# Layer 2 of a four-layer graph network: weights times values by one level of Strassen's method

## The chip, the cores and the metric

The kernel runs on one core of one Trainium2 chip. The metric is the device time of one execution in microseconds (us), smaller being better. Several executions were timed; one more was profiled.

In the profile PE is TensorE's matmul, PEld its weight load (which runs beside PE), DVE is VectorE, ACT is ScalarE, POOL is GpSimd and SP is SyncE, whose queue issues nearly all DMAs here. L977 is line 977 of the kernel before.

## What is computed

A graph of N = 3327 nodes with 256 features each goes through four layers. Each layer adds its output to its input and normalizes the rows. All arithmetic is f32. Layer 2, cut to what matters:

```python
q = x @ Wq.T + bq
k = x @ Wk.T + bk
v = x @ Wv.T + bv
scores = q @ k.T / sqrt(256)
scores = where(adj > 0, scores, -9e15)
attention = softmax(scores, axis=-1)
att = attention @ v
x = layernorm(x + elu(att))
```

Layers 0, 1 and 3 have the same core, a masked softmax of N x N weights times N x 256 values. Layer 0's weights come from a cosine similarity. In layer 1, and in the three graph attention layers that make up layer 3 (called 3a, 3b and 3c in the kernel), a weight comes from a sum of one term per row and one per column, without a matmul of scores.

## The kernel before

N is padded to 26 tiles of 128 nodes. The queries are cut into 7 blocks b: six of 512 (four tiles) and a last one of 256 (two tiles). The main loop goes over steps (layer, b, j), j being one of the 26 tiles of keys.

For each step, `make` builds the weights of tile j against block b, a tile e of 128 keys x 512 queries. In layer 2 that is `weights2` (line 489 on): two calls of the score matmul (line 498, 512 columns each), an exp on ACT (line 506) and a multiplication by the 0/1 mask on DVE (line 425, in `masked`). In the graph attention layers it is a Relu on ACT (line 591) and an operation on DVE (line 599). `make` runs LA = 2 steps ahead of the products.

The products are line 977: for each of the block's four query tiles k, the 128 x 128 part of e is the stationary operand and V[j], 128 keys x 257 columns, streams past it into PSUM. Column 257 of V is 1, so that the last column of the result is the sum of the weights. The four results `pos` lie in one PSUM bank each, from a pool of five banks (`ps_o`); three more banks (`ps_b`) serve scores and everything else. A block adds up over its 26 tiles of keys.

When a block is done, `finish` divides by the sum (lines 720 to 724: a max and a reciprocal on DVE, a scaling on ACT), applies the nonlinearity, adds the input, normalizes, and prepares what the next layer needs. It is a generator: the main loop advances it one piece per step, so that this work lies beside the next block's products. In layer 1 it also turns the rows (a DMA transpose), and computes the values of layer 2 with the matmul of line 846. A generator `block2` computes the query side of the next block of layer 2 (`gT`) from j = 14 on. `Sum` gathers the mean of the values, which is written into the row of the one padded node at the end of a layer (lines 639 to 647).

The masks of a block, 1.7 MB, are fetched by one DMA per block. The setups of layers (`setup1`, `setup2`, `setup3a`, `setup3`) load and combine weight matrices; `setups` runs them in pieces during layer 0 from block 1 on.

Past the first four steps, the tile framework's scheduler orders the instructions of each engine by its own estimates, so the order on an engine isn't that of the source. Buffers come from pools: a tag with `bufs=n` has n buffers, and a new tile waits until its buffer's last user is done. Among the tags concerned, `x4k` has two buffers, shared by xT, gT, the transposes' planes and pT4; `e` has five; `acc` has one.

Of the kernel before, what the change touches and what calls it, by code (L numbers as in the profile page):

```python
# [8 lines left out]
F32 = mybir.dt.float32  # L9
# [21 lines left out]

@with_exitstack
def gnn_stack(ctx: ExitStack, tc: tile.TileContext, a: dict, N: int, out: bass.AP):

# [53 lines left out]
    for k in range(4):  # L90
        nc.tensor.matmul(turned[:, :P], count, part, start=(k == 0), stop=(k == 3))
    ident = const.tile([P, P], F32, name="ident")
    nc.vector.tensor_tensor(ident, turned[:, :P], count, ALU.is_equal)
    ispad = ident[:, P - 1 : P]
    notpad = const.tile([P, 1], F32, name="notpad")
    nc.vector.tensor_scalar(notpad, ispad, -1.0, 1.0, ALU.mult, ALU.add)


    V = [
# [7 lines left out]

    s_d = [dram.tile([1, bw(b)], F32, name=f"s_d{b}") for b in range(NB)]
    a_d = {k: dram.tile([1, 4 * P], F32, name=f"a_d{k}") for k in ("1", "3a", "3b", "3c")}
    x_d = {  # L110
        k: [dram.tile([P, D], F32, name=f"x{k}_d{t}") for t in range(NT)]
        for k in ("2", "3c")
# [45 lines left out]
    def gat_rows(key, wt, v):  # L158

        c = wts.tile([P, 4], F32, tag="wa", name="wa")  # L160
        nc.scalar.copy(
            c.rearrange("p (i f) -> p f i", i=2),
            times(wt, v).rearrange("p (f i) -> p f i", i=2),
        )
        yield
        pr = bank("prt")
        nc.tensor.transpose(pr[:4, :P], c, ident)
        rt = wts.tile([4, P], F32, tag="rt", name="rt")
        nc.scalar.copy(rt, pr[:4, :P])
        nc.sync.dma_start(a_d[key].rearrange("o (c n) -> (o c) n", n=P), rt)  # L170
        r = wts.tile([P, 2, D], F32, tag="row_" + key, name="row_" + key)
        nc.sync.dma_start(
            r.rearrange("p i n -> p (i n)"),
            a_d[key].rearrange("o n -> (o n)").partition_broadcast(P),
        )
        w["row_" + key] = r
# [71 lines left out]
        yield  # L248
        yield from gat_rows("3a", w0t, c)

    def setup3(key, n):
        w[key] = load_w(f"l3_w{n}")
        wt = load_w(f"l3_w{n}t", wts, "scratch1")
        v = load_a(key)
        yield
        yield from gat_rows(key, wt, v)

    def setups():
        for g in (setup1(), setup2(), setup3a(), setup3("3b", 2), setup3("3c", 3)):
            yield from g  # L260
            yield

# [120 lines left out]
    def take_adj(b, j):  # L383

        wd = bw(b)
        st = stages.pop((b, j))[:, : 2 * wd]
        nc.vector.tensor_scalar(mask(b, j, 2), st, 0, None, ALU.is_gt)  # L387
        if j == 0:
            adj_sum[b] = st
        elif j == 2:  # L390
            acc = work.tile([P, 2 * CH], I32, tag="acc", name="acc", bufs=1)
            acc = acc[:, : 2 * wd]
            nc.vector.tensor_tensor(acc, adj_sum[b], st, ALU.add)
            adj_sum[b] = acc
        else:
            acc = adj_sum[b]
            nc.vector.tensor_tensor(acc, acc, st, ALU.add)  # L397
# [209 lines left out]
            return e  # L607


    def turn(x4, n, out):  # L610

        half = "p k (n t) -> p t k n"
        pl = work.tile([P, 4, 2, D], U16, tag="x4k", name="planes", bufs=2)
        for t in range(2):
            nc.scalar.copy(pl[:, :n, t, :], x4[:, :n, :].bitcast(U16).rearrange(half, t=2)[:, t])  # L617
        yield
        tr = work.tile([P, 16, P], U16, tag="stage", name="turned", bufs=3)
        nc.sync.dma_start_transpose(  # L620
            out=tr[:, : 4 * n, :], in_=pl[:, :n].rearrange("p k t n -> p (k t n)")
        )
        for _ in range(3):
            yield
        trv = tr[:, : 4 * n, :].rearrange("p (k t h) i -> p t k h i", t=2, h=2)
        for t in range(2):
            nc.vector.tensor_copy(out(t), trv[:, t])  # L627
        yield
# [19 lines left out]
    def finish(L, b, pos):  # L648
# [21 lines left out]
        if L.key == "0":  # L670
# [15 lines left out]

            z0 = cols.tile([P, 4], F32, tag="z0", name="z0")
            nc.vector.tensor_scalar(z0[:, :n], z_[:, :n], 0.1, None, ALU.is_lt)
            if b == NB - 1:
                nc.vector.tensor_tensor(  # L690
                    z0[:, n - 1 : n], z0[:, n - 1 : n], notpad, ALU.mult
                )
            c2 = cols.tile([P, 4], F32, tag="c2", name="c2")
            nc.vector.tensor_scalar(c2[:, :n], am, -1.0, 2.0, ALU.mult, ALU.add)
            for k, t in enumerate(ts_):
# [19 lines left out]
                    yield  # L715
        else:
            p4 = work.tile([P, 4, D], F32, tag="stage", name="p4", bufs=3)
            for k, t in enumerate(ts_):
                ri = cols.tile([P, 1], F32, tag="ri", name="ri", bufs=4)
                nc.vector.tensor_scalar(  # L720
                    ri, pos[k][:, D : D + 1], TINY, None, ALU.max
                )
                nc.vector.reciprocal(ri, ri)
                nc.scalar.mul(p4[:, k, :], pos[k][:, :D], ri)  # L724
            if L.key in x_d:
                x4 = work.tile([P, 4, D], F32, tag="stage", name="x4", bufs=3)
                xr = [x4[:, k, :] for k in range(4)]
# [77 lines left out]
        if not L.hidden:  # L805
# [29 lines left out]
            if L.key == "1":  # L835
# [7 lines left out]
                for k, t in enumerate(ts_):  # L843
                    pm = bank("pv")
                    for h in range(2):
                        nc.tensor.matmul(  # L846
                            pm[:, :D],
                            FT[b][:, h, k * P : (k + 1) * P],
                            w["v"][:, h, :],
                            start=(h == 0),  # L850
                            stop=(h == 1),
                        )
                    nc.vector.tensor_tensor(nxt[t][:, :D], pm[:, :D], w["bv"], ALU.add)
                    if k % 2:
                        yield
                dsts = [nxt[t][:, :D] for t in ts_]
            for k in range(0, n, 2):
                follow((k, k + 1), dsts)
# [3 lines left out]
            L.gat_next.rows(b)  # L862
        if b == NB - 1:
            L.sum.close(nxt[NT - 1])
            if L.gat_next is not None:
                L.gat_next.keys(ts_[0], NT)
        elif b == NB - 2 and L.gat_next is not None:
            L.gat_next.shift(ts_[-1] + 1)
            yield
            L.gat_next.keys(0, ts_[-1] + 1)  # L870
# [36 lines left out]
    def make(s):  # L907
        if s >= len(steps):
            return
        L, b, j = steps[s]  # L910
        if L.is_gat:
            made.append(L.gat.weights(b, j))
        else:
            made.append((weights0 if L.key == "0" else weights2)(b, j))

    for i in range(2):
        for t in range(NT):
# [21 lines left out]
    for s, (L, b, j) in enumerate(steps):  # L939
        last = L.key == "3c"  # L940
        first = L.key == "0" and b == 0
        if j == 0:
            pos = [
                ps_o.tile([P, D + 1], F32, tag="po", name="po") for _ in tiles_of(b)
            ]
        if first:

            g, part = (j + 4) // 4, j % 4
# [24 lines left out]
            next(prep[0])  # L973
        else:
            make(s + LA)
        for k in range(len(pos)):
            nc.tensor.matmul(  # L977
                pos[k],
                made[0][:, k * P : (k + 1) * P],
                V[L.i % 2][j],  # L980
                start=(j == 0),
                stop=(j == NT - 1),
            )
        made.popleft()
        if s == 3:
            start.__exit__(None, None, None)
        if L.key == "0" and j == NT - 1 - LA:
# [5 lines left out]
        elif j == 8 and not (last and b == NB - 1):  # L993
            nb = (b + 1) % NB
            masks[nb] = fetch_mask(nb)
        if L.key == "0" and b >= 1 and j % 3 == 1:
            next(setup, None)
        nl, nb = (L, b + 1)
        if nb == NB:
# [87 lines left out]
```

## Time and profile before

| what | us |
|---|---|
| median of 3 runs | 2434.77 |
| lowest and highest | 2433.78, 2436.84 |
| span of the profiled execution | 2434.4 |
| DVE, ACT busy | 1411.9, 1008.5 |
| products of line 977, PE busy, all layers (8112 records) | 1841.6 |
| scores of line 498, PE busy (728 records) | 320.4 |
| first and last score record of layer 2 start at | 847.6, 1454.0 |

The profile notes each f32 matmul call as two records, each with its own weight load. The length of a record on PE is modelled and longer than its share of the time, since matmuls overlap: 380 ns for a record of 257 columns. The distance from one record's start to the next is the time that it costs.

The granted TensorE clock was 0.995 of full speed over the span. In the 40 slices of the page PE is at nine tenths or more in all but the first and the last.

### The profile page before, as it was taken

The numbers are of one execution on the slowest core, as the hardware profiler recorded it, in microseconds if no ns is written. First come the engines' busy times: TensorE is split into PE (matmuls) and PEld (weight loads), VectorE is DVE, ScalarE is ACT, GpSimd is POOL, SyncE is SP. The second block draws the span as 40 slices with busy tenths as digits, with TensorE's granted clock in tenths as the row PEclk, the third lists the DMA queues.
The fourth block names the chain that finished last, engine by engine and source line by source line (L and its number), as shares of the span: only waits on it lengthen the run. The fifth ranks groups of instructions, "written<-read, shape, count | busy, mean of one in ns | idle before, by whom it ended". The sixth has DMA issues, their size and how long they took to land.

```text
span 2434.4 us, 27870 instructions
## 1 busy us (share of the span) xinstructions
PE 2397.5 (98%) x10117; PEld 1901.3 (78%) x10117; DVE 1411.9 (58%) x3625; ACT 1008.5 (41%) x1692; POOL 5.4 (0%) x65
## 2 busy tenths in 40 slices
PE   8999999999999999999999999999999999999997
PEld 6777777788888766666666688888888888888886
DVE  7567776666666634244244256655656655655665
ACT  4422222255555422222222245555465555655553
POOL 0000000000000000000000000000000000000000
PEclk9999999999999999999999999999999999999999
DMA  8145434222221301011010021111121111123121
GB/s 277 65 141 162 132 101 135 100 76 71 68 59 52 90 13 46 5 50 46 1 46 32 1 71 54 42 49 52 48 70 50 42 42 58 46 83 84 59 60 26
DMA packets 119998, 164.67 MB, mean 68 GB/s; under 512 B 73149, under 2 KB 97972, under 8 KB 115252
## 3 DMA queue, kind: packets, MB, share of 16 engines
q1 hardware_dynamic: 119588, 162.63, 21.6%
q8 instruction: 79, 1.29, 0.2%
q14 instruction: 59, 0.48, 0.1%
q10 hardware_dynamic: 272, 0.26, 0.0%
HBM read 124.72 MB, written 21.36 MB: 60 GB/s over the span
## 4 chain that ended last, share of the span: by engine, by line
PE 95%; DVE 3%; DMA 1%; issue 0%; ACT 0%; DVEq 0%; ACTq 0%
PE po L977 70%; PE ps L498 12%; PE ps L436 5%; PE pproj L765 4%; PE pv L846 1%; PE pgq L457 1%; DMA stage<-in_adj_a 1%; PE pqk L306 0%; DVE acc L397 0%; DVE ejunk L525 0%; DVE mask L387 0%; DVE e L425 0%; DVE e L599 0%; DMA turned<-planes 0%; PE pqkT L347 0%
## 5 line engine op out<-in xcount | busy, mean ns | idle before, releaser
L977 PE MATMUL po<-v,e 128*128 128x257 f32 x8112 | 1841.6, 380 | 6.1 <-DVE e L599 3.1
L977 PEld LDWEIGHTS po<-v,e 128*128 128x128 f32 x8112 | 1537.3, 190 | 363.9 <-issue 128.5
L591 ACT ACTIVATE re<-u,nrh,th 128x512 f32<-128x512 f32 (+1 forms) x728 | 554.7, 780 | 518.3 <-DVE e L599 470.3
L599 DVE SCALAR_TENSOR_TENSOR e<-re,rh,mask 128x512 f32<-128x512 f32 (+1 forms) x728 | 513.5, 709 | 400.4 <-PE po L977 386.6
L425 DVE SCALAR_TENSOR_TENSOR e<-ex,mask 128x512 f32<-128x512 f32 (+1 forms) x364 | 236.0, 649 | 438.6 <-ACT ex L506 325.3
L498 PE MATMUL ps<-gT,ft 128*128 128x512 f32 (+1 forms) x728 | 320.4, 562 | 0.0
L506 ACT ACTIVATE ex<-ps,off 128x512 f32<-128x512 f32 (+1 forms) x182 | 119.4, 656 | 400.9 <-PE ps L498 387.4
L445 ACT ACTIVATE ex<-ps 128x512 f32<-128x512 f32 (+1 forms) x182 | 103.1, 566 | 262.2 <-PE ps L436 239.6
L498 PEld LDWEIGHTS ps<-gT,ft 128*128 128x128 f32 x728 | 137.4, 190 | 90.0 <-issue 79.4
L436 PE MATMUL ps<-ft,ft 128*128 128x512 f32 (+1 forms) x312 | 150.2, 565 | 0.8 <-ACT ft L351 0.7
L397 DVE CUSTOM_DVE_ANT_0 acc<-acc,stage 128x2048 uint16<-128x2048 uint16 (+1 forms) x77 | 87.4, 1135 | 0.1
L765 PE MATMUL pproj<-w_l_w,pT 128*128 128x256 f32 x312 | 79.2, 381 | 3.2 <-DVE pT L627 1.7
L775 ACT ACTIVATE elu_e<-elu_e 128x256 f32<-128x256 f32 x130 | 53.0, 408 | 39.4 <-DVE elu_e L774 39.4
L765 PEld LDWEIGHTS pproj<-w_l_w,pT 128*128 128x128 f32 x312 | 58.7, 190 | 13.0 <-DVE pT L627 3.1
L387 DVE TENSOR_SCALAR mask<-stage 128x1024 uint8<-128x1024 int32 (+1 forms) x91 | 58.4, 642 | 17.9 <-DMA stage<-in_adj_a 15.6
L436 PEld LDWEIGHTS ps<-ft,ft 128*128 128x128 f32 x312 | 57.2, 191 | 10.2 <-ACT ft L351 0.9
L724 ACT ACTIVATE p<-po,ri 128x256 f32<-128x256 f32 x130 | 54.2, 464 | 8.0 <-PE po L977 6.7
L639 DVE TENSOR_TENSOR xsum<-xsum,v 128x256 f32<-128x256 f32 (+1 forms) x130 | 54.4, 418 | 1.5
L617 ACT COPY planes<-p 128x1024 uint16<-128x1024 uint16 (+1 forms) x54 | 51.2, 995 | 0.7
L774 DVE TENSOR_SCALAR elu_e<-pproj 128x256 f32<-128x256 f32 x104 | 42.7, 410 | 6.9 <-PE pproj L765 5.6
L627 DVE COPY pT<-turned 128x1024 uint16<-128x1024 uint16 (+1 forms) x54 | 35.2, 706 | 17.1 <-DMA turned<-planes 17.1
L790 DVE SCALAR_TENSOR_TENSOR y<-elu_e,y 128x256 f32<-128x256 f32 x78 | 32.5, 418 | 20.0 <-ACT elu_e L775 19.4
(147 smaller groups left out, 892.1 us busy)
## 6 DMA issues: line engine op xcount, KB each, us to landing
mask<-mask_d SPq DMA_DIRECT2D x30, 1664.0 KB
stage<-in_adj_a SPq DMA_DIRECT2D x78, 512.0 KB
mask_d<-mask SPq DMA_DIRECT2D x6, 1664.0 KB
u<-s_d SPq DMA_DIRECT2D x24, 256.0 KB
mask<-mask_d SPq DMA_DIRECT2D x5, 832.0 KB
v<-in_x SPq DMA_DIRECT2D x26, 128.0 KB
stage<-in_adj_z SPq DMA_DIRECT2D x13, 256.0 KB
x_d<-o SPq DMA_DIRECT2D x26, 128.0 KB
```

The source lines that it names most:

```text
L387: nc.vector.tensor_scalar(mask(b, j, 2), st, 0, None, ALU.is_gt)
L397: nc.vector.tensor_tensor(acc, acc, st, ALU.add)
L425: nc.vector.scalar_tensor_tensor(e[:, :wd], t_[:, :wd], 0.0, mask(b, j), ALU.add, ALU.mult)
L436: nc.tensor.matmul(ps[:, :wd], FT[j // 4][:, 0, (j % 4) * P : (j % 4 + 1) * P], FT[b][:, 1, :wd], start=True, stop=True,)
L445: nc.scalar.activation(t_[:, :wd], ps[:, :wd], AF.Exp)
L498: nc.tensor.matmul(ps[:, :wd], FT[j // 4][:, h, (j % 4) * P : (j % 4 + 1) * P], g[:, h, :wd], start=(h == 0), stop=(h == 1),)
L506: nc.scalar.activation(t_[:, :wd], ps[:, :wd], AF.Exp, bias=off, scale=1.0 / D**0.5)
L591: nc.scalar.activation(t_[:, :wd], self.u[b][:, :wd], AF.Relu, bias=self.nrh[:, j : j + 1], scale=self.th[:, j : j + 1],)
L599: nc.vector.scalar_tensor_tensor(e[:, :wd], t_[:, :wd], self.rh[:, j : j + 1], mask(b, j), ALU.add, ALU.mult,)
L639: nc.vector.tensor_tensor(self.acc[:r], self.acc[:r], x[:r], ALU.add)
L765: nc.tensor.matmul(pm[:, :D], pT[:, h, :], w[L.w][:, h, :], start=(h == 0), stop=(h == 1),)
L977: nc.tensor.matmul(pos[k], made[0][:, k * P : (k + 1) * P], V[L.i % 2][j], start=(j == 0), stop=(j == NT - 1),)
```

## The change

In layer 2, the products are made for two key tiles at a time. For a pair p of key tiles (values b1 and b2) and a block of queries, the weights e1 and e2 are split into halves by queries and the values into halves by columns. Seven products of half blocks, by Strassen's method in Winograd's form, take the place of eight. For a full block each product is two matmul calls (one per query tile of the half) of 128 columns, or of 129 where the column of ones goes along: products 1, 2 and 5.

- `combine` forms four sums of value halves per pair on DVE during layer 1's finish, and writes them to DRAM (`t_d`, 128 x 513). `fetch_tsum` fetches a pair's sums for every block, into three buffers.
- `sums2` forms four sums of weight halves per pair and block on DVE, into the `acc` buffers, of which there are now two.
- `products2` issues the seven products, and `places` says where their results lie: in four whole banks, also for the half block.
- `joined2` adds the seven results up into the four quarters of the output, once per block; the scaling then reads these from SBUF.

Outside layer 2: the setup of 3b moves from layer 0 to layer 1 and that of 3c to layer 3a, each from block 1 on, and they take over the buffers of other weights (tags `w_l0_wqk`, `w_l1_w`, `row_1`, `row_3a`). A correction for the padded node in layer 0 (`notpad`) is dropped.

```diff
+    t_d = [dram.tile([P, 4 * H + 1], F32, name=f"t_d{p}") for p in range(NT // 2)]
...
-            acc = work.tile([P, 2 * CH], I32, tag="acc", name="acc", bufs=1)
+            acc = work.tile([P, 2 * CH], I32, tag="acc", name="acc", bufs=2)
...
+    def combine(p, v):
+        b1, b2 = v[2 * p], v[2 * p + 1]
+        b11, b12, b21, b22 = b1[:, H:D], b1[:, :H], b2[:, H:D], b2[:, :H]
+        t = work.tile([P, 4 * H + 1], F32, tag="x4k", name="tsum", bufs=2)
+        t1, t2, t3, t4 = (t[:, c : c + H] for c in (0, H + 1, 2 * H + 1, 3 * H + 1))
+        nc.gpsimd.memset(t[:, H : H + 1], 1.0)
+        nc.vector.tensor_tensor(t1, b12, b11, ALU.subtract)
+        nc.vector.tensor_tensor(t2, b22, t1, ALU.subtract)
+        nc.vector.tensor_tensor(t3, b22, b12, ALU.subtract)
+        nc.vector.tensor_tensor(t4, t2, b21, ALU.subtract)
+        nc.sync.dma_start(t_d[p], t)
...
+    def fetch_tsum(b, p):
+        t = work.tile([P, 4 * H + 1], F32, tag="tsum", name="tsums", bufs=3)
+        nc.sync.dma_start(t, t_d[p])
+        tsums[b, p] = t
+
+    def sums2(b, e1, e2):
+        hw = bw(b) // 2
+        x = work.tile([P, 4, D], F32, tag="acc", name="ssum", bufs=2)
+        s1, s2, s3, s4 = (x[:, i, :hw] for i in range(4))
+        e11, e21 = e1[:, :hw], e1[:, hw : 2 * hw]
+        e12, e22 = e2[:, :hw], e2[:, hw : 2 * hw]
+        nc.vector.tensor_tensor(s3, e11, e21, ALU.subtract)
+        nc.vector.tensor_tensor(s1, e21, e22, ALU.add)
+        nc.vector.tensor_tensor(s2, s1, e11, ALU.subtract)
+        nc.vector.tensor_tensor(s4, e12, s2, ALU.subtract)
+        return e11, e12, e22, s1, s2, s3, s4
...
+    def places(pos, b):
+        o = H + 1
+        m = {
+            1: ((0, 0, o), (0, o, o)),
+            2: ((0, 2 * o, o), (1, 0, o)),
+            5: ((1, o, o), (1, 2 * o, o)),
+            3: ((2, 0, H), (2, H, H)),
+            4: ((2, D, H), (2, D + H, H)),
+            6: ((3, 0, H), (3, H, H)),
+            7: ((3, D, H), (3, D + H, H)),
+        }
...
+        for k, x, y in (
+            (1, e11, b1[:, H:]),
+            (2, e12, b2[:, H:]),
+            (4, e22, t[:, 3 * H + 1 :]),
+            (7, s3, t[:, 2 * H + 1 : 3 * H + 1]),
+            (5, s1, t[:, : H + 1]),
+            (6, s2, t[:, H + 1 : 2 * H + 1]),
+            (3, s4, b2[:, :H]),
+        ):
+            for i, (g, o) in enumerate(where[k]):
+                todo.append((g, o, x[:, i * P : (i + 1) * P], y))
...
+        for i, (g, o, x, y) in enumerate(todo):
+            nc.tensor.matmul(
+                o,
+                x,
+                y,
+                start=(p == 0 and g not in banks[:i]),
+                stop=(p == NT // 2 - 1 and g not in banks[i + 1 :]),
+            )
...
+    def joined2(pos, b, c):
...
+        for i in range(q):
+            nc.vector.tensor_copy(z[:, i : i + 1], w_[1][i][1][:, H:])
+            nc.vector.tensor_tensor(
+                z[:, i : i + 1], z[:, i : i + 1], w_[2][i][1][:, H:], add
+            )
+            nc.vector.tensor_copy(z[:, q + i : q + i + 1], w_[5][i][1][:, H:])
+        nc.scalar.copy(c22, both(1))
+        for i in range(q):
+            nc.vector.tensor_tensor(c[:, i, H:], c22[:, i], w_[2][i][1][:, :H], add)
+        nc.vector.tensor_tensor(c22, c22, both(6), add)
+        nc.vector.tensor_tensor(c21, c22, both(7), add)
+        nc.vector.tensor_tensor(c12, c22, both(5), add)
+        nc.vector.tensor_tensor(c22, c21, both(5), add)
+        nc.vector.tensor_tensor(c21, c21, both(4), sub)
+        nc.vector.tensor_tensor(c12, c12, both(3), add)
...
-            if b == NB - 1:
-                nc.vector.tensor_tensor(
-                    z0[:, n - 1 : n], z0[:, n - 1 : n], notpad, ALU.mult
-                )
...
+        if L.key == "2" and j % 2 == 0:
+            fetch_tsum(b, j // 2)
...
+            if L.key == "2" and j % 2:
+                e2, e1 = made.pop(), made.pop()
+                made.append(None)
+                made.append(sums2(b, e1, e2))
...
-            pos = [
-                ps_o.tile([P, D + 1], F32, tag="po", name="po") for _ in tiles_of(b)
-            ]
+            wo, no = (CH, 4) if L.key == "2" else (D + 1, len(tiles_of(b)))
+            pos = [ps_o.tile([P, wo], F32, tag="po", name="po") for _ in range(no)]
...
+        elif j % 2:
+            products2(pos, b, j // 2, es, V[L.i % 2])
...
+        if (b, j) == (1, 0):
+            if L.key == "1":
+                setup = setup3("3b", 2, "w_l0_wqk")
+            elif L.key == "3a":
+                setup = setup3("3c", 3, "w_l1_w")
+        if b >= 1 and j % 3 == 1:
             next(setup, None)
```

## The prediction

> **What bounds the kernel now.** I read the page's busy shares first, then the chain of waits, then layer 2 alone (about 848 to 1454 us: the span in which the score matmuls of line 498 run): busy times by stretch, and the timeline of single instructions.
>
> ```profile
> PE 2397.5 (98%) x10117; PEld 1901.3 (78%) x10117; DVE 1411.9 (58%) x3625; ACT 1008.5 (41%) x1692; POOL 5.4 (0%) x65
> ...
> PE 95%; DVE 3%; DMA 1%; issue 0%; ACT 0%; DVEq 0%; ACTq 0%
> ```
>
> TensorE carries 95% of the chain. Busy time alone would not prove that it is limited, so I look at one block of layer 2 and two pairs of key tiles in it:
>
> ```profile
> 950.00:1040.00 90.00, 90.00 (x313) 58.74 (x312) 33.26 (x99) 21.08 (x35) 0.00 (x0) 1.00 0.07 20
> ...
> 944.37 1.90 PE L977 MATMUL po<-v,e 128*128 128x257 f32 x8
> 946.10 1.88 PE L498 MATMUL ps<-gT,ft 128*128 128x512 f32 x4
> 947.82 1.90 PE L977 MATMUL po<-v,e 128*128 128x257 f32 x8
> ```
>
> PE is busy 90.00 of 90 us, DVE 33.26, ACT 21.08, DMA 7%. Each matmul call leaves two records, so "x8" is the four calls of one key tile. Start to start, eight take 946.10 - 944.37 = 1.73 us (216 ns each); from the row's own length, less the last one's 0.38, (1.90 - 0.38) / 7 = 217. I take 216.7. Four score records take 1.72 us, 430 ns each. There is no gap between rows: in layer 2, the time is the sum of TensorE's start-to-start times. So the question is what a half-as-wide product costs, and whether anything new makes PE wait.
>
> A 128-column weight load has its own pace. Three places show it:
>
> ```profile
> 119.48 0.75 PEld L149 LDWEIGHTS pr<-a,w_l_wt 128*128 128x128 f32 x6
> ...
> 5.89 0.19 PEld L91 LDWEIGHTS turned<-part,count 128*128 128x128 f32 x1
> 6.00 0.19 PEld L306 LDWEIGHTS pqk<-w_l_wqk,xT 128*128 128x128 f32 x1
> ...
> 13.35 0.27 PEld L347 LDWEIGHTS pqkT<-ident,qk 128*128 128x128 f32 x2 [0.57 <-ACT qk L316]
> ```
>
> Line 149 streams two columns per record, so loads alone set its pace: (0.75 - 0.19) / 5 = 112 ns, though one "lasts" 190. Between the loads at 5.89 and 6.00 a 128-wide f32 matmul of line 91 runs: 0.11 us again. The transposes at 13.35 take 0.27 - 0.14 = 0.13 us, the 0.14 being one such load, but these wait for data.
>
> [...] the next weights load while the current matmul runs; that is what the 217 ns pace beside 190 ns loads shows. [...] line 639's row has 418, so I use 418[...]. [...]
>
> **The change part by part.** *Products.* Removed: 26 x 26 = 676 calls of 257 columns, 1352 records x 216.7 ns = 293.0 us. Added: 14 calls for each of 13 pairs in six full blocks (1092) and 7 in the half block (91), 1183 calls, 2366 records of 128 or 129 columns. The stream scales as 216.7 x 128/257 = 108 ns, less than the 112 of the load: a record now costs its load. I take 111.5: 263.8 us. Net -29.2, all on the path. Bounds: 109 ns a record if the load hid wholly (-35), 133 as the transposes (+22). Seven eighths of the arithmetic thus becomes nine tenths of the time.
>
> *Sums of weights.* DVE gets 312 adds of 256 columns x 0.418 and 52 of 128 x 0.291: 130 + 15 = 146 us over layer 2. A pair lasts 3.43 (scores) + 28 x 0.1115 = 6.55 us; DVE has two masks of 0.69 and four adds, 3.05. Latency: from the pair's last score, exp 0.69, mask 0.69, three adds 1.25, some 0.3 of hand-overs: 2.9 us. The order of the built kernel puts the former pair's products (3.12) and the next pair's scores (3.43) in between, 6.55. Hidden. The two buffers of sums make DVE wait for the products of two pairs earlier, long done; behind it stand the next masks.
>
> *Sums of values.* 52 adds x 0.291 = 15 us on DVE in layer 1, where it is busy some 33 of 50 us: hidden by line 977's matmuls. 13 column memsets go to an idle POOL; 13 writes of 263 KB and 91 fetches go to SP's queue, 13 fetches per block beside 10 to 11 transfers. An issue takes some 0.3 to 0.4 us; a same-sized read (u, issued at 1086.17, packets to 1089.0) 2.9 us, and 24 MB over 577 us is 41 GB/s beside bursts of 339. Three buffers let a fetch start two pairs (13 us) ahead. Once per block one is queued behind a 1.7 MB mask (6.3 us from issue): 9.2 us, still ahead. The exception is pair 12 in block 0: it needs the mean row and the block's old gT buffer, and is written and read back behind a mask. From the order: mask issued 8.1 us before block 0's nominal end, written by +0.3, read by +3.2, wanted at +1.9: +1.3 us. All other PE queues behind that wait.
>
> *Joining.* Per block the removed max and reciprocal of each tile (0.31 x 4) make room for six column operations (0.15), an ACT copy (0.47) and eight adds, about 4.5 us of DVE. PE has the next block's scores for key tiles 2 and 3 (3.43) and the first products in the one spare bank before it needs an old one. Laying DVE's order out with these durations, S being the end of the second score group: banks free at S+4.4, 6.4 and 7.2, wanted at 7.5, 7.5 and 7.9. Hidden, with 0.3 to 1 us to spare. Into layer 3a there are no scores to hide behind, and the half block now holds four banks instead of two: the second tile waits to S+5.8 for S+4.9, the third 0.9 more: +1.9 us. At layer 2's start DVE makes two value sums before the first weights (8 x 0.291): +0.3. Slips in seven boundaries: +1.0.
>
> *Moved setup.* 3b goes from layer 0 to layer 1 and 3c to layer 3a, from block 1 on: each 5 small PE calls (under 1 us), two ACT copies, three loads, a write and a broadcast on SP. The same work on the same path elsewhere: nothing. SP there carries u, masks and transposes, each due many us later. Two pad instructions fewer at the start (0.15 us each) and a second acc buffer: nothing, since line 977 covers layer 0's DVE after the first 50 us; the altered order in those is worth 0.5 either way.
>
> Sum: -29.2 + 1.3 + 1.9 + 0.3 + 1.0 = -24.7. On the profiled span of 2434.4 that is 2409.7; the runs' median, 2434.77, lies 0.4 above that span, so **2410**.
>
> **The rivals.** *A, the sum above.* For it: the zero idle time of PE and the 111 ns beside a real 128-wide matmul. Against: few such records exist, and of a different line.
>
> *B, VectorE decides locally.* Over a block DVE is not the bound: 33 + 52 x 0.418 + about 3.5 = 59 of 86 us. But the last block's finishing (about 20 us of DVE, strict order) sits between the masks and sums of a block's first pairs, where my layout leaves 2.3 us. If one 0.42 us operation too many stands ahead in six pairs of each block, 6 x 0.42 x 6.5 = 16 us: 2426.
>
> *C, the fetches come late.* If the one behind the mask misses by 3 us in seven blocks, 21: 2431. Against it stand 13 us of lead.
>
> *D, slower.* TensorE's load does not keep 112 ns here: nearly every new call carries a wait at its load, its outputs start at odd columns, and loads read fresh sums. Place: line 687 of the changed kernel; price: the transposes' 133 ns, 2366 x 0.133 = 314.7, +21.7 + 4.5: 2461. It decides from (293.0 - 4.5) / 2366 = 122 ns on. Against: loads with a wait now start as promptly behind the former matmul as those without, though at 217 ns a delay up to 100 would be hidden.
>
> **How the numbers follow.** A 0.66 (own range 2403 to 2418: 109 ns, or 5 us more of slips), B 0.15, C 0.05, D 0.14. 2403 to 2430 holds nearly all of A and most of B and C, 0.80; D is left out. Within 0.2% (4.9 us, about what a measurement of this kernel can tell from no change) lie only tails of B and C: 0.06. Faster 0.80, slower 0.14.
>
> **What would show it.** Right: in a block of layer 2, 14 product calls whose loads start 111 to 112 ns apart, 6.55 us from pair to pair, blocks near 86 us instead of 93.5, and idle PE of a few us at layer 2's ends. D would show as 122 ns or more with no named releaser; B as PE waiting for the sums on DVE; C as PE waiting for the fetched sums. A layer other than 2 changed by over 2 us would make the reasoning wrong even at the right time.

## The result, and the profile after

| | before | after |
|---|---|---|
| median of 4 runs, us | 2434.93 | 2417.17 |
| lowest and highest | 2433.78, 2436.84 | 2416.21, 2417.64 |
| span of the profiled execution | 2434.4 | 2414.4 |
| DVE busy | 1411.9 | 1570.2 |

The ratio is 0.9926, with a 95% interval of 0.9909 to 0.9943: faster by 17.8 us. The forecast was 2410, 7 us lower.

First the page of the kernel after: busy shares, the chain that ended last, and the rows of line 687, which now makes layer 2's products (columns: group and count, busy us and mean ns of one, idle us before them).

```profile
PE 2372.8 (98%) x11131; PEld 1908.9 (79%) x11131; DVE 1570.2 (65%) x4095; ACT 1010.5 (42%) x1699; POOL 12.8 (1%) x78
...
PE 92%; DVE 4%; DMA 2%; ACT 1%; issue 1%; SPq 0%; DVEq 0%; POOL 0%; ACTq 0%
...
L687 PE MATMUL po<-tsums,ssum 128*128 128x128 f32 (+1 forms) x1014 | 128.3, 275 | 0.0
...
L687 PE MATMUL po<-v,e 128*128 128x129 f32 x676 | 90.6, 275 | 0.4 <-DVE e L426 0.4
...
L687 PE MATMUL po<-tsums,e 128*128 128x128 f32 x338 | 52.6, 275 | 1.7 <-DMA tsums<-t_d 1.7
```

TensorE is still 98% busy, and the idle time that these rows show before its products is little: 1.7 us for a fetched sum of values, 0.4 for a mask on DVE. The means of 275 ns are modelled and overlap, so the pace has to be read from starts. The same stretch of a block as before, 950 to 1040 us (busy us of PE, PEld, DVE, ACT, POOL, clock, DMA share, GB/s):

```profile
950.00:1040.00 90.00, 90.00 (x489) 63.19 (x489) 59.96 (x179) 24.87 (x44) 0.00 (x0) 1.00 0.25 75
```

DVE has gone from 33.26 to 59.96 us of 90, DMA from 7% to 25%, and PE still never idles. Then the timeline of one pair on PE, from its products to the next pair's:

```profile
1004.97 1.05 PE L687 MATMUL po<-v,e 128*128 128x129 f32 x8
1005.86 0.61 PE L687 MATMUL po<-tsums,e 128*128 128x128 f32 x4
1006.30 1.50 PE L687 MATMUL po<-tsums,ssum 128*128 128x128 f32 x12
1007.64 0.61 PE L687 MATMUL po<-v,ssum 128*128 128x128 f32 x4
1008.09 0.28 PE L481 MATMUL pn<-g,ones 128*128 128x1 f32 x2
1008.24 3.68 PE L499 MATMUL ps<-gT,ft 128*128 128x512 f32 x8
1011.75 1.05 PE L687 MATMUL po<-v,e 128*128 128x129 f32 x8
```

The 28 product records start at 1004.97 and are done with at 1008.09: 3.12 us, 111.4 ns each, where 111.5 was forecast. No row ends before the next begins. (This pair also holds two small records of line 481.) And the same records as weight loads:

```profile
1006.20 1.42 PEld L687 LDWEIGHTS po<-tsums,ssum 128*128 128x128 f32 x12
```

(1.42 - 0.19) / 11 = 112 ns, the pace that line 149 had shown before. Taken over all of layer 2, the distances from start to start of line 687's 2366 records have a median of 112 ns and, waits left out, a sum of 264.4 us against a forecast of 263.8.

Where the 17.8 us come from is told by the moment at which a layer's last results (or the first block's of layer 3a) are first read on DVE. Each column is the stretch up to that moment, from one profiled execution of each kernel. All but before and after belong to experiments that follow; after_again is a second profile of the kernel after.

| profile | to the end of layer 0 | layer 1 | layer 2, to 3a's first block | rest of 3a | 3b | 3c and end | span |
|---|---|---|---|---|---|---|---|
| before | 505.4 | 346.7 | 649.6 | 274.2 | 321.7 | 336.8 | 2434.4 |
| before_turn (differs in 3c only) | 503.7 | 346.7 | 649.7 | 274.2 | 321.3 | 336.7 | 2432.3 |
| after | 503.9 | 347.3 | 624.9 | 275.2 | 322.1 | 341.0 | 2414.4 |
| after_again | 503.5 | 346.9 | 625.4 | 275.3 | 322.0 | 339.3 | 2412.4 |
| rest_only | 504.2 | 346.4 | 649.6 | 275.2 | 321.9 | 339.2 | 2436.5 |
| setup_only | 502.2 | 348.4 | 649.6 | 275.2 | 321.6 | 338.0 | 2435.0 |
| direct_turn | 503.4 | 347.2 | 623.0 | 275.2 | 321.8 | 338.1 | 2408.7 |

Layer 2 gained 649.6 - 624.9 = 24.7 us, the sum of the prediction (24.2 in the second profile of the same kernel). After it, 1.0 + 0.4 + 4.2 = 5.6 us were lost again (3.9 in the second profile), where none had been forecast. The experiments ask two things: is the weight load really what sets the pace, and where do the lost microseconds come from?

### The profile page after: what moved, and what is told of

Same layout as the page of the kernel before. It is cut to its first block, busy times and chain, and to the rows that moved or that the text cites. A ratio compares the mean times of both kernels' runs of the same rounds, so it can differ in the third digit from the quotient of the medians.

```text
span 2414.4 us, 30688 instructions
## 1 busy us (share of the span) xinstructions
PE 2372.8 (98%) x11131; PEld 1908.9 (79%) x11131; DVE 1570.2 (65%) x4095; ACT 1010.5 (42%) x1699; POOL 12.8 (1%) x78
## 4 chain that ended last, share of the span: by engine, by line
PE 92%; DVE 4%; DMA 2%; ACT 1%; issue 1%; SPq 0%; DVEq 0%; POOL 0%; ACTq 0%
PE po L1113 57%; PE ps L499 12%; PE po L687 11%; PE ps L437 5%; PE pproj L889 4%; DMA stage<-in_adj_a 1%; PE pv L970 1%; PE pgq L458 1%; DVE mask L388 1%; DVE acc L398 1%; DMA turned<-planes 0%; DVE ejunk L526 0%; PE pqk L307 0%; DVE e L426 0%; DVE e L600 0%
## 5 line engine op out<-in xcount | busy, mean ns | idle before, releaser
L1113 PE MATMUL po<-v,e 128*128 128x257 f32 x6760 | 1520.3, 381 | 6.4 <-DVE e L600 3.1
L1113 PEld LDWEIGHTS po<-v,e 128*128 128x128 f32 x6760 | 1279.5, 190 | 262.7 <-issue 61.8
L499 PE MATMUL ps<-gT,ft 128*128 128x512 f32 (+1 forms) x728 | 307.6, 563 | 0.0
L499 PEld LDWEIGHTS ps<-gT,ft 128*128 128x128 f32 x728 | 132.0, 190 | 114.0 <-issue 110.9
L687 PE MATMUL po<-tsums,ssum 128*128 128x128 f32 (+1 forms) x1014 | 128.3, 275 | 0.0
L687 PEld LDWEIGHTS po<-tsums,ssum 128*128 128x128 f32 x1014 | 120.7, 192 | 0.0
L687 PEld LDWEIGHTS po<-v,e 128*128 128x128 f32 x676 | 89.9, 191 | 38.1 <-issue 31.8
L687 PE MATMUL po<-v,e 128*128 128x129 f32 x676 | 90.6, 275 | 0.4 <-DVE e L426 0.4
L687 PE MATMUL po<-tsums,e 128*128 128x128 f32 x338 | 52.6, 275 | 1.7 <-DMA tsums<-t_d 1.7
```

The costliest lines, as they stand in the source:

```text
L499: nc.tensor.matmul(ps[:, :wd], FT[j // 4][:, h, (j % 4) * P : (j % 4 + 1) * P], g[:, h, :wd], start=(h == 0), stop=(h == 1),)
L687: nc.tensor.matmul(o, x, y, start=(p == 0 and g not in banks[:i]), stop=(p == NT // 2 - 1 and g not in banks[i + 1 :]),)
L1113: nc.tensor.matmul(pos[k], es[:, k * P : (k + 1) * P], V[L.i % 2][j], start=(j == 0), stop=(j == NT - 1),)
```

## The experiments

**Is it the load?** Two kernels vary one side of a product each, a third both.

half_stream: the same loads, half the columns streamed.

```diff
+            c = 0 if p == 0 else H // 2
             nc.tensor.matmul(
-                o,
+                o[:, c:],
                 x,
-                y,
+                y[:, c:],
```

> The changed kernel, but each product of layer 2 streams only its last 64 (or 65) columns, except in pair 0; half of these sums is left out. Theory (the weight load sets the pace of a 128-column product): records of line 687 stay 112 ns apart, time as the changed kernel, 2417 +- 3 us. Rival (the stream or a fixed cost per streamed column sets it): records near 56 ns, 2184 x 56 = 122 us less, about 2295 us.

Measured: 2413.32 us (2411.01 to 2414.24), ratio 0.9911 [0.9898, 0.9925]. Layer 2 took 624.7 us, as in the kernel after, though by a balance of small things: the wait of 1.9 us for a fetched sum, of which more below, is missing, while about 1.5 us at half clock and 0.5 us of waits in the half block are new. The pace decides. A part of a pair, as PE row and weight loads:

```profile
1010.56 1.50 PE L688 MATMUL po<-tsums,ssum 128*128 128x64 f32 x12
...
1010.51 1.42 PEld L688 LDWEIGHTS po<-tsums,ssum 128*128 128x128 f32 x12
```

Half the columns, and both rows are as long as those of the kernel after, 1.50 and 1.42 us. The rival is out by over 100 us: here the stream is hidden by the load of 128 columns.

half_load: half the columns of weights loaded (x[:, c:] in place of x, for pairs 1 to 11), all columns streamed. Half of the rows of a sum then get nothing from these pairs; the least value allowed for the sum of the weights is raised to 1.

```diff
+            c = 0 if p in (0, NT // 2 - 1) else H // 2
             nc.tensor.matmul(
-                o,
-                x,
+                o[c:, :],
+                x[:, c:],
                 y,
...
-                nc.vector.tensor_scalar(z, z, TINY, None, ALU.max)
+                nc.vector.tensor_scalar(z, z, 1.0, None, ALU.max)
```

> The changed kernel, but in pairs 1 to 11 each product of layer 2 loads only 64 of its 128 columns of weights and streams its 128 or 129 columns past them; half of the rows of these sums is left out (2002 records). Theory (the load of 128 columns is the floor, just above the stream): records fall from 112 to the stream's 109 (128 columns x 0.843 = 108 by the 257-column records), 6 us less. Rival (some fixed cost of a matmul, not the load, makes the 112): still 112 ns.

Measured: one run, 2443.63 us, so 27 us slower than the kernel after (about 2416), not 6 faster. The records came near to what the theory said; their neighbours didn't. Loads of one pair, then PE rows from its end to the next pair's start:

```profile
1004.36 1.34 PEld L688 LDWEIGHTS po<-tsums,ssum 128*64 128x64 f32 x12
```

```profile
1005.79 0.60 PE L688 MATMUL po<-v,ssum 128*64 128x128 f32 x4
1006.32 1.98 PE L458 MATMUL pgq<-ft,G 128*128 128x512 f32 x4
1008.14 3.60 PE L499 MATMUL ps<-gT,ft 128*128 128x512 f32 x8
1011.66 1.09 PE L688 MATMUL po<-v,e 128*64 128x129 f32 x8
```

One load now lasts 0.14 us, so the pace is (1.34 - 0.14) / 11 = 109 ns: the stream's. But the four records at 1005.79 take 0.53 us to the next row, 0.09 more than 4 x 0.109; the four score-sized records at 1006.32 take 1.82 us, 0.10 more than four of 0.43; and the eight at 1008.14 take 3.52 us, 0.09 more than 3.43. Besides, the first record of a visit to 64-column weights takes 0.05 us more than the others (161 for 110 ns). So each visit costs some 0.34 us. Line 688 is entered at this width 95 times: 32 us. The gaps at the way in and the way out are 93 ns each in the median; no run shows what causes them. The pace gives some 4 us back (110 ns in the median for 112, in 2002 records). In the half block, waits for the sums are longer (3.4 us for 1.6), and about 1.5 us were lost at half clock behind them; the 1.9 us for a fetched sum are missing here too. Together that is 30 us; layer 2 took 653.7 us for 624.9, 28.8 more.

half_both: both edits together.

> As the one above, and each product streams only its last 64 or 65 columns, so that both are halved. Theory (the longer of load and stream sets the pace, both in proportion to columns): records near 56 ns, 2002 x 56 = 112 us less, about 2304 us, a little more if VectorE then is late in places. Rival (a fixed cost per matmul): 112 ns and no less time.

Measured: one run, 2341.12 us, 75 us less than the kernel after. Loads of one pair:

```profile
1001.05 0.78 PEld L688 LDWEIGHTS po<-tsums,ssum 128*64 128x64 f32 x12
```

(0.78 - 0.14) / 11 = 58 ns. So in these runs the pace is the longer of load and stream (112 ns with 128 columns loaded and 128 or 64 streamed, 109 with 64 loaded and 128 streamed, 58 with 64 of each), and at half the columns neither takes more than about half as long; no fixed cost of a matmul makes the 112. 2002 x 54 ns = 108 us, plus the 1.9 of the missing wait, less 32 for the changes of width, 3 for longer waits in the half block and 2 at half clock there, is 73; layer 2 took 71.5 us less (553.4 for 624.9).

**Where TensorE waits.** Two of the new waits were taken away one at a time.

no_fetch: the sums of value halves gone, with their writes and fetches (combine and fetch_tsum are not called).

```diff
-            (4, e22, t[:, 3 * H + 1 :]),
-            (7, s3, t[:, 2 * H + 1 : 3 * H + 1]),
-            (5, s1, t[:, : H + 1]),
-            (6, s2, t[:, H + 1 : 2 * H + 1]),
+            (4, e22, b2[:, :H]),
+            (7, s3, b1[:, :H]),
+            (5, s1, b1[:, H:]),
+            (6, s2, b2[:, :H]),
```

> The changed kernel without the sums of value halves: none is formed, written or fetched; plain halves of the values stand in their place. Theory: only the one wait in block 0 (1.9 us) goes, 2415 us. Rival C (late fetches or their traffic cost more): 2412 us or less. If the writes and fetches are what delays the transposes at the end or the layers after, the loss after layer 2 shrinks too.

Measured: 2412.31 us (2411.29 to 2414.09), ratio 0.9909 [0.9896, 0.9923]. The time lies near the rival's bound, but the trace doesn't bear the rival out: layer 2 took 623.7 us, 1.2 to 1.7 less than in the two profiles of the kernel after, and the one wait that is gone is the one at block 0's last pair. In the kernel after this reads (1.9 us by the distance from start to start):

```profile
944.71 0.83 PE L687 MATMUL po<-v,e 128*128 128x129 f32 x6
947.27 0.71 PE L687 MATMUL po<-tsums,e 128*128 128x128 f32 x4 [1.73 <-DMA tsums<-t_d]
```

91 fetches in layer 2, and one was late. The layers after lost as much as with the fetches (the last column is 339.7, that of after_again 339.3), so this traffic isn't what delays them.

one_sum: three of the four sums of weight halves gone.

```diff
-        s1, s2, s3, s4 = (x[:, i, :hw] for i in range(4))
+        s1 = x[:, 0, :hw]
-        nc.vector.tensor_tensor(s3, e11, e21, ALU.subtract)
+        s2, s3, s4 = e12, e21, e22
         nc.vector.tensor_tensor(s1, e21, e22, ALU.add)
-        nc.vector.tensor_tensor(s2, s1, e11, ALU.subtract)
-        nc.vector.tensor_tensor(s4, e12, s2, ALU.subtract)
```

> The changed kernel with one of the four sums of weight halves (s1); plain halves stand in for the other three, 273 VectorE operations fewer. Theory (the sums lie beside TensorE's work but for the half block's 1.6 us): 2415 to 2416 us, idle TensorE at the half block gone. Rival B (VectorE decides locally in more places): 2412 us or less.

Measured: 2412.87 us (2411.14 to 2413.7), ratio 0.9909 [0.9894, 0.9924], below what the theory said and above what the rival said. Layer 2 took 623.2 us, 1.7 to 2.2 less: what the half block's waits (0.60, 0.22 and 0.79 us, by the distances from start to start) and one of 0.47 us at layer 3a's entry were, all of which are gone. In the kernel after, PE and DVE in the half block:

```profile
1405.51 0.39 PE L687 MATMUL po<-v,e 128*128 128x129 f32 x2
1406.33 0.49 PE L687 MATMUL po<-v,e 128*128 128x129 f32 x2 [0.44 <-DVE e L426]
...
1408.93 0.27 PE L570 MATMUL psr<-ident,sd 128*4 128x128 f32 x1 [0.63 <-DVE sd L526]
```

```profile
1405.17 0.42 DVE L526 CUSTOM_DVE_ANT_0 ejunk<-v,row_3a 128x256 f32<-128x256 f32 x1
...
1405.51 0.42 DVE L526 CUSTOM_DVE_ANT_0 ejunk<-v,row_3a 128x256 f32<-128x256 f32 x1
...
1405.86 0.42 DVE L426 SCALAR_TENSOR_TENSOR e<-ex,mask 128x256 f32<-128x256 f32 x1
```

The row terms of layer 3a (line 526) stand ahead of the mask for which PE waits. That is mechanism B, but in one place and of 1.6 us. In the other blocks PE shows no gap over 0.15 us but the one for the fetched sum. So B as forecast (16 us) falls.

half_stream, no_fetch and one_sum all ended 4 to 5 us below the first measurement of the kernel after, though layer 2 explains at most 2. So that kernel was measured once more.

> The changed kernel once more. If its 4 us above the three variants without some of its work (2411 to 2413 us) is the changed kernel's own, it is 2416 to 2418 us again and the profile shows 3.4 us of half clock near the last block again; if that was chance, 2412 to 2415 us and no half clock there. The wait of 2 us or more for the transposed rows in front of the last block is expected again (all variants had 1.3 to 2.3, the kernel before 0.7).

Measured: 2415.75 us (2414.22 to 2417.3), ratio 0.9921 [0.9909, 0.9934]; the nine times of both measurements run from 2414.22 to 2417.64 with a median of 2416.21. That lies between the two cases expected; 1 to 2 us of the three variants' lead stay unexplained. The wait of about two microseconds near the end came again, the half clock behind it did not. Both show in the stretch of 2360 to 2395 us, first in the kernel after, then in its second run (after_again); the clock is the third number from the right:

```profile
2360.00:2395.00 35.00, 32.88 (x145) 28.23 (x144) 21.85 (x71) 17.33 (x33) 0.00 (x0) 0.95 0.13 32
```

```profile
2360.00:2395.00 35.00, 32.41 (x149) 27.61 (x147) 22.33 (x76) 17.84 (x34) 0.00 (x0) 1.00 0.15 38
```

0.95 over 35 us is 3.4 us at half clock; it began 1.1 us after the end of a wait of PE of 2.28 us (here and below by the distance from start to start, 2.12 by the profile's idle time), and 8 records took some 0.21 us more each, 1.7 us. In the second run PE waited there for 2.12 us and the clock stayed. The records of the granted clock show a grid. In the kernel before it is at half from 43.41 to 53.65 us and from 2422.50 us on; in the kernel after from 43.48 to 50.30, from 2378.19 to 2381.61 and from 2402.09 us on. The stretches that end within the span last 10.24, 6.83 and 3.41 us, three, two and one times 3413.3 ns, and the later ones begin 697, 684 and 691 times 3413.3 ns after the first of their profile. Cut into periods on this grid, the wait in the kernel after lay inside one of them (2374.78 to 2378.19 us, 2.12 us of it idle), while in after_again a border cut it, leaving at most 1.13 us of idle time in a period. Past the first 115 us of these two profiles and up to the period in which PE's last record ends, the three with 2.12, 2.12 and 2.28 us of idle PE (by the modelled ends of its records) were followed by half clock, and the others, with up to 1.73 us, were not. Over the fourteen traces, cut the same way, all periods with 1.84 us or more were followed by it, and those with up to 1.82 us were not, but for two of 1.22 and 1.42 us in half_stream and half_both. So, as far as these traces tell, 1.7 us of the first measurement's profile hang on where the wait fell on the grid, and the rest doesn't; no run moves the wait alone.

**The wait near the end.** In layer 3c, the rows of the last full block are turned by a DMA, and the half block's on TensorE. The wait, in the kernel before and in the kernel after (in rest_only, below, PE was idle for 1.82 us there):

```profile
2393.11 2.92 SPq L620 DMA_TRANSPOSE turned<-planes  x1
...
2397.38 1.36 DVE L627 COPY pT<-turned 128x1024 uint16<-128x1024 uint16 x2 [0.72 <-DMA turned<-planes]
...
2398.80 1.56 PE L765 MATMUL pproj<-w_l_w,pT 128*128 128x256 f32 x6 [0.56 <-DVE pT L627]
```

```profile
2369.89 1.79 SPq L741 DMA_TRANSPOSE turned<-planes  x1
...
2375.71 1.36 DVE L748 COPY pT<-turned 128x1024 uint16<-128x1024 uint16 x2 [2.28 <-DMA turned<-planes]
...
2377.12 1.13 PE L889 MATMUL pproj<-w_l_w,pT 128*128 128x256 f32 x4 [2.12 <-DVE pT L748]
```

From the transposes' issue to the copy that needs them it took 2397.38 - 2393.11 = 4.27 us before and 5.82 us after, with a fetch of instructions, one packet of 16 KB, on the DMA engines beside it in both. Two kernels turn that block's rows on TensorE instead.

pe_turn (before_turn: the same line in the kernel before):

```diff
-            final = L.key == "3c" and b == NB - 1
+            final = L.key == "3c" and b >= NB - 2
```

> The changed kernel, but the rows of layer 3c's last full block are transposed on TensorE, as those of its half block are, not by DMA. Theory: the wait of 2.3 us and what half clock follows it go, some eight transposes of about 0.25 us and their hand-overs come: 1 to 3 us less than the changed kernel. Rival (the wait is only shifted, TensorE idles for the transposes' copies instead): no less.

> The kernel before with the same edit of layer 3c. Its wait there was 0.7 us: about 2434 to 2436 us. If the edit gains as much here as in the changed kernel (over 1 us), the wait at this place is not something the change brought.

Measured: pe_turn 2413.86 us (2413.27 to 2416.36), 1.9 less than the kernel after on the same chip (2415.75), though the runs overlap; no gap of PE over 0.3 us is left there. before_turn 2435.06 us (2433.81 to 2436.61) against 2434.64 for the kernel before, 1.0002 [0.9994, 1.001]: nothing gained. By these runs, what can be gained there is new with the change. As to why the transposes land later: their last packet landed 3.8 us after issue before and 4.8 after, and the fetch of instructions differs in its place. Before, it was over 1.39 us after the issue, when the transposes' packets had hardly begun (at 1.18); after, it ran from 3.67 to 4.55 us, among their last. This holds more widely. Of the 416 DMA transposes of full blocks in the fourteen traces, the 330 without a fetch of instructions between 1.2 and 4.3 us after the issue took 4.31 us to their reader in the median and 4.70 at most; the 86 with one took 4.68 in the median and up to 6.04. In the nine profiles of kernels with the moved setups that turn this block by DMA it took 4.66 to 5.88 us. So a fetch of instructions among the packets goes along with a late landing; no run moves the fetch alone, and why it falls there in these kernels was not followed up.

**What the rest of the change costs.** rest_only is the changed kernel without sums2, combine, fetch_tsum, products2 and joined2; setup_only is the kernel before with nothing but the setups moved.

```diff
-        for g in (setup1(), setup2(), setup3a(), setup3("3b", 2), setup3("3c", 3)):
+        for g in (setup1(), setup2(), setup3a()):
...
-        if L.key == "0" and b >= 1 and j % 3 == 1:
+        if (b, j) == (1, 0):
+            if L.key == "1":
+                setup = setup3("3b", 2, "w_l0_wqk")
+            elif L.key == "3a":
+                setup = setup3("3c", 3, "w_l1_w")
+        if b >= 1 and j % 3 == 1:
```

> The changed kernel with layer 2's products, sums and joining as before: what stays is the setups of 3b and 3c moved into layers 1 and 3a, no notpad, and two acc buffers. Layer 2 gave 24.7 us between the two traces, the runs only 17.7, so 7 are lost elsewhere. Theory 1 (the rest of the change loses them: records of the setup where TensorE is never idle, masks and transposes moved): 2439 to 2442 us. Theory 2, as predicted (moved setup costs nothing; what is lost after layer 2 comes by the products' new timing or by chance): 2434 to 2436 us.

> The kernel before with the setups of 3b and 3c moved to layers 1 and 3a, and nothing else of the change. Theory (the move is what the rest of the change loses): 2435.5 to 2437 us, 1 us more in 3a's second block and 1 us less in layer 0. Rival (the two acc buffers or the dropped correction lose it): 2434 to 2435 us.

Measured: rest_only 2436.48 us (2435.11 to 2438.27), ratio 1.0009 [1.0001, 1.0017], so 2.3 us slower; setup_only 2436.78 us (2435.45 to 2438.12), ratio 1.0008 [1.0000, 1.0016], so 1.7 us slower, by an interval that reaches to no difference at all. Neither theory had the size right for rest_only: by its median the rest of the change loses a third of what was to be explained. By its profile, of the slowest of its 13 runs, layers 3a to 3c lose 1.0 + 0.2 + 2.4 = 3.6 us, nearly the 3.9 of after_again. By the medians the moved setups lose most of it; the second acc buffer and the dropped correction were not taken apart. The table shows where. In setup_only, layer 3a has 1.0 us more, as in every profile with the moved setups (275.2 us or more for 274.2). PE's groups in its second block (1500 to 1552 us), setup_only first, before second:

```profile
L978 PE MATMUL po<-v,e 128*128 128x257 f32 x219 | 49.1, 381 | 0.0
...
L149 PE MATMUL pr<-a_3c,w_l_w3t 128*128 128x2 f32 x8 | 0.9, 241 | 0.0
L167 PE MATMUL prt<-ident,wa 128*4 128x128 f32 x1 | 0.3, 273 | 0.0
```

```profile
L977 PE MATMUL po<-v,e 128*128 128x257 f32 x224 | 49.9, 381 | 0.0
```

Nine small records of the setup, at their load's 112 ns, put five products out of the stretch: 9 x 0.112 = 1.0 us. TensorE is never idle there, so the small records are paid in full. What layer 0 gains by their leaving is hidden in its scatter: 505.4 and 503.7 us in the two profiles with these setups in it, 502.2 to 505.1 in the twelve without. Layer 1 took 3b's, but its +1.7 in setup_only holds a late transpose as well; in rest_only it is -0.3. What stands out is 3c: 336.8 and 336.7 us before, 337.9 or more in all twelve. In setup_only it is +1.2, of which 0.7 at the entry, where PE lost 0.92 us beyond its pace for 0.26 in the kernel before, and 0.4 in front of the last block (1.11 for 0.73). PE's wait at the entry, setup_only:

```profile
2099.17 2.00 PE L978 MATMUL po<-v,e 128*128 128x257 f32 x8 [0.75 <-ACT p L725]
```

and on ACT, ahead of that scaling of line 725, setup_only first, before second:

```profile
2098.03 0.72 ACT L584 ACTIVATE u<-u,ub 128x512 f32<-128x512 f32 x1 [0.85 <-DMA u<-s_d]
```

```profile
2097.91 0.72 ACT L583 ACTIVATE u<-u,ub 128x512 f32<-128x512 f32 x1 [0.20 <-DMA u<-s_d]
```

PE waits for a bank, the bank for its scaling on ACT, and the scaling stands behind an exp that waits for u. On SP's queue, u is issued ahead of the next block's 1.7 MB mask in both: 0.78 us ahead before, 0.52 us after the move, and u then takes 5.06 us from issue to its reading instead of 4.40. The other profiles say the same: 0.52 us ahead and 4.79 to 5.47 in all twelve with the move, 0.77 and 4.22 in before_turn. That the mask's packets delay it is a reading of the trace; no run separates the two. The changed products with the setups left in layer 0, which would have shown the move from the other side, were not tried.

**Both remedies.** direct_turn forms pair 12's sums of values straight in the buffer that block 0 reads (`finish` no longer does it), and has the edit of pe_turn.

```diff
     def fetch_tsum(b, p):
         t = work.tile([P, 4 * H + 1], F32, tag="tsum", name="tsums", bufs=3)
-        nc.sync.dma_start(t, t_d[p])
+        if (b, p) == (0, NT // 2 - 1):
+            combine(p, V[layers[2].i % 2], t)
+        else:
+            nc.sync.dma_start(t, t_d[p])
```

> The edit of layer 3c as above, and pair 12's sums of value halves are formed in the buffer from which block 0 reads them, in place of a write and a read back. Theory: the 1.9 us wait at layer 2's first boundary goes, 1 to 2.5 us less than with the first edit alone. Rival (the adds now stand between the masks and sums of block 0's last pairs on VectorE): TensorE waits there as long, no less.

Measured: 2410.77 us (2410.51 to 2411.76), ratio 0.9902 [0.9888, 0.9915]; 3.1 us less than pe_turn, 5.0 less than the kernel after on the same chip, and no run of it reaches theirs. Layer 2 took 623.0 us for pe_turn's 624.9: the 1.9 us wait. (The two profiles differ by another 1.4 us in layer 0, in which the kernels are alike.) At that place the rows now follow without a gap:

```profile
946.47 1.05 PE L691 MATMUL po<-v,e 128*128 128x129 f32 x8
947.36 0.61 PE L691 MATMUL po<-tsums,e 128*128 128x128 f32 x4
```

half_plain is direct_turn with the half block multiplied as before the change. Where the products are chosen:

```diff
+            fast = L.key == "2" and b < NB - 1
-            wo, no = (CH, 4) if L.key == "2" else (D + 1, len(tiles_of(b)))
+            wo, no = (CH, 4) if fast else (D + 1, len(tiles_of(b)))
...
-        if L.key != "2":
+        if not fast:
```

> The changed kernel with both remedies (transposes of the last full block on TensorE, pair 12's sums formed in place), and with the half block of layer 2 multiplied as before the change, in eight products. By the sum, the half block's products cost 13 x (8 x 216.7 - 14 x 112) ns = 2.2 us more, while its waits for VectorE (1.6 us) and some 0.5 us at layer 3a's entry go: 2410.5 to 2412 us, no gain. Rival (the half block's sums and four banks cost more than that): 2409.5 us or less.

Measured: 2411.2 us (2410.77 to 2414.06), ratio 0.9906 [0.9892, 0.9919]; layer 2 took 622.8 us for 623.0. No gain and no loss, as the sum said: in the half block, the products' gain of 2.2 us is about what its waits and those at layer 3a's entry cost (2.1). The highest of its four times, 2414.06 us, is the profiled one: there two transposes of layer 3b landed late (5.95 and 6.04 us, each with a fetch of instructions among its packets), and PE waited 1.08 and 2.49 us for them, where direct_turn has no such wait at the one place and one of 0.75 at the other. direct_turn is the fastest of the kernels that compute the whole.

## Why the prediction was right, and where it was off

- *Products.* Right. 111.5 ns a record was forecast, 112 is the median, and 264.4 us stand for 263.8. That the load and not the stream sets it was read off line 149 and is now shown (half_stream, half_load, half_both). D, the slower case, had argued that waits at the loads would show; records with a wait fall into the same 112 ns, and the 133 ns of the transposes did not come back.
- *Sums of weights.* Hidden, as forecast, in six blocks of seven. DVE's share over a block came out as 59.96 of 90 us. In the half block they are not: 1.6 us. The forecast had put 1.0 us of slips at the boundaries; those between full blocks had none, and the half block, with half the scores to hide behind, had 1.6 us inside. Forecast at 0.418 us for 256 columns and 0.291 for 128, the adds of the kernel after took 0.42 us (lines 642 to 645) and 0.285 to 0.293 (the same lines in the half block, and lines 622 to 625); the kernel before has one add of 128 columns, of 0.292 us (line 93).
- *Sums of values.* One late fetch, at the place named: 1.9 us for the 1.3 forecast. C is out: the other 90 cost no wait.
- *Joining.* Hidden at the boundaries between blocks. The 1.9 us forecast for the entry to layer 3a were 0.7 (0.19 and 0.47): too much, and by luck it made up for the half block.
- *Blocks "near 86 us".* Wrong as a figure: full blocks take 89.05 us. 13 x 6.55 = 85.2 left out what else PE does in a block (projections, the next block's gT). The difference to before, 93.5 - 89.05 = 4.45, is right: 208 x 216.7 - 364 x 111.5 ns = 4.49.
- *Moved setup: "nothing".* This step failed. setup_only took 1.7 us more in the median. Layer 3a paid 1.0 us for 3c's records, with no matching gain that shows in layer 0. And the order on SP's queue shifted: the prediction took u, masks and transposes there as "each due many us later", but PE waits for u at layer 3c's entry, 0.9 us in setup_only for 0.3 before. The prediction's own mark said so: 3c changed by 4.2 us, where it had set 2 as the point from which the reasoning is wrong for a layer other than 2.
- *The end.* Not in the prediction at all: the wait for the turned rows of the last full block grew by 1.4 to 1.6 us in the two profiles, and in the first 1.7 us at half clock followed it.
- *From span to time.* The sum was set against the profiled span, and the median taken as 0.4 us above it. But a time lies 1.8 us above its own span: the profiled run of before took 2436.18 us, 1.4 above the median of 2434.77 that was known, and that of after 2416.21, 1.0 below its own. This makes 2.4 us of the 7.2. The other 4.7 are 5.6 lost after layer 2, less 0.9 gained ahead of it (503.9 + 347.3 against 505.4 + 346.7).

So the mechanism of case A holds, and its sum for layer 2 is exact to the tenth, partly because two misses inside it cancel. What stays open is why, with the moved setups, a fetch of instructions falls among the packets of the DMA transpose near the end, and whether it is this that makes them late.

## What to carry to other kernels

Before counting saved multiplications, price one narrow product by the slower of its weight load and its stream: here an f32 record of 128 columns costs its 112 ns load and not its 109 ns stream, so that seven eighths of the arithmetic came out as nine tenths of the time. Where TensorE is never idle, as in layer 3a here, small records moved to another stage are paid in full there (nine of them, 1.0 us), and the order and spacing on the DMA queue change around them; a wait of a microsecond can then appear layers away (0.92 us for 0.26 at layer 3c's entry, in setup_only). Set a predicted difference against medians through the profiled run's own time, not through its span.

## What the runs showed of the hardware that was not expected

- In half_load, going from 128-column weights to 64-column ones and back cost TensorE 0.09 us at each change, 0.05 more in the first record behind the way in and 0.10 in the first wide one behind the way out: 0.34 us a visit, 32 us in all, where the shorter loads gained 4.
- The stretches at half clock began at whole multiples of 3413.3 ns from the first of them (684, 691 and 697 of them in the kernels after and before) and, where they ended within the span, lasted 3.41, 6.83 or 10.24 us. They came after periods of this grid in which PE was idle for 2.12 us or more in these two kernels, and for 1.84 us or more over all fourteen traces (for less in two cases, where the streams were half as wide). A wait of 2.28 us inside one period was followed by 3.4 us at half clock; waits of 2.12, 2.34 and 2.30 us at the same place in after_again, no_fetch and one_sum, each cut by a border of the grid into pieces of at most 1.29 us of idle time, were not.
- The same DMA transpose took 4.3 us from issue to its reader in most cases and up to 6.04; all but one of those over 4.6 us had a fetch of instructions of 8 or 16 KB among their packets.
